# A graph layer by Strassen products on one core: VectorE's order written out, with sums of blocks two steps ahead

## The chip, the core and the metric

The kernel runs on one core of a Trainium2 chip. A core has five engines with a queue of instructions each: PE (TensorE, the matmuls), DVE (VectorE), ACT (ScalarE), POOL (GpSimd) and SP (SyncE). SP, ACT and POOL issue the DMAs. The metric is the device time of one execution in microseconds (us), the median of several runs. Beside it there is one profiled execution, whose instructions carry times; its span runs from the first to the last instruction.

## The reference, cut

There are 4096 nodes with 512 features in x, and a symmetric adjacency `adj` of 4096 x 4096 with nonzero values at some 0.8% of its places.

```python
# layer 0: a dense product with the scaled adjacency
h = relu(layernorm(x))
d = rowsum(adj) ** -0.5
x = x + relu((d[:, None] * adj * d[None, :]) @ h @ W0 + b0)
# layer 1: attention over the nonzero places, with both signs
h  = relu(layernorm(x))
hw = h @ W1
e  = leaky_relu(hw @ a[:512] + (hw @ a[512:]).T, 0.2)
p  =  softmax(where(adj > 0,  e, -1e12))
q  = -softmax(where(adj > 0, -e, -1e12))
x  = x + elu(concat([p @ h, q @ h], 1) @ wtrans)
```

## The kernel before, in words

**The work.** Layer 0 is done densely. `y0` holds h times W0, scaled by d, for all 4096 nodes in 32 tiles of 128 rows. The output's 32 row tiles are made in nine groups of four or two tiles: `GROUPS` is (28,4), (16,4), (26,2), (20,4), (0,4), (4,4), (8,4), (12,4), (24,2), as (first tile, number). Group 0 is an ordinary product that is done while x and adj are read and normalized, up to 312 us of the profiled span. Groups 1 to 8 (312 to 1059 us) use Strassen's method in Winograd's form: seven products in place of eight, over 16 steps `jp` of two row tiles of `y0` each. Layer 1 is sparse: per block of nodes it gathers the rows of a table (POOL, L473), and weights and sums them; it runs from group 8 to the end of the span.

**A step of a group** has these parts. `load_at` has SP load a block of adj. `sum_at` (L953) has DVE make four sums of its quarter blocks (L959 to L962) into a tile "sums", of which three buffers exist. `multiply_blocks` (L965) issues 28 matmuls of 128 x 256 (14 in a group of two tiles), all from L972. `pack` has ACT make the mask of nonzero places (L812), which POOL stores to the table (L821) once for two steps. In group 1 alone, `sum_y` (L938) also has DVE make the sums of the blocks of `y0`, which the later groups use again.

**The end of a group** is done during the next one. `take` is `join_blocks` (L846): DVE joins the seven products of a pair of tiles out of PSUM (L854 to L864), which frees the banks for the new group, and scales them (`affine`, L834). Then each finished row tile passes through `finish0` (L884): DVE adds x (L887), POOL stores the tile (L888, "x1d") and clears three columns of h (L889), DVE takes mean and variance and three small operations (L705, L706, L708) around a square root on ACT (L707), ACT makes h by a relu (L711), DVE makes two dot products with the attention vectors (L895), and the row tile is put in eight tables (L465): in one by POOL, in the seven others by ACT. h has two buffers. When all tiles of a group are through, `spread_s` (L907) turns their dot products on PE (L910, `s_ps`), and ACT copies and stores them.

**The lists.** For the sparse layer DVE also makes lists of nodes by class, in two halves (g = 1, then g = 0), each with seven classes. `list_round` (L397) finds eight entries with MAX8 (L410) and strikes them with MATCH_REPLACE (L412); a half has 73 rounds. A finished class gives a tile `li` (L425, two buffers), and eight `join`s (L428): indirect DMAs issued by POOL (L432), 56 for a half. `deal` (L439) has POOL fetch the whole list (L442), PE transpose it in three parts (L449) and DVE keep it (L450). `make_places` (L633) works out offsets, from a small product on PE (its DVE copy is L669).

**What sets the order.** The kernel is written in program order, and a scheduler sets the order of each engine's queue, except where `keep_in_program_order` fixes an instruction. `group` (L1118) is a loop over the steps: it prepares the blocks of step jp + 1, joins the former group at step 0, multiplies step jp, packs, finishes a tile of the former group in steps 0 to 3 (0 and 1 after a group of two), spreads s at step 12, and calls `step(jp)` (L1182), which takes so many pieces from the two lists `listing` and `joining`:

```python
n = 0 if b == 2 or not 0 < jp < 14 else 1 if b == 1 else 2 + jp % 2
for todo, n in ((listing, n), (joining, 1 + jp % 2)):
    for _ in range(n):
        if todo:
            todo.pop(0)()
```

Group 8 is called with other pools, after the lists are done.

Of the kernel before, what the change touches and what calls it, by code (L numbers as in the profile page):

```python
# [8 lines left out]
F32 = mybir.dt.float32  # L9
# [10 lines left out]
P = 128  # L20
# [12 lines left out]
NE = 8  # L33
# [234 lines left out]
def gcn_gat_kernel(  # L268
# [55 lines left out]
    def bank(name):  # L324
        return ps.tile([P, 512], F32, tag="ps", name=name)
# [112 lines left out]

    def deal(g):  # L439

        rows = make_pool.tile([P, EN], F32, tag="flag16", name=f"deal{g}")[:, : NH * STR // P]
        i = nc.gpsimd.dma_start(  # L442
            out=rows.rearrange("r (c p) -> r c p", p=P),
            in_=lst_dram[g].rearrange("(c r p) o -> r c (p o)", r=P, p=P),
        )
        turned = bank(f"deal_ps{g}")
        for c in range(NH * STR // P // P):
            part = slice(c * P, (c + 1) * P)
            nc.tensor.transpose(turned[:, part], rows[:, part], ident)  # L449
        nc.vector.tensor_copy(idx[g].rearrange("p b k -> p (b k)"), turned[:, : NH * STR // P])  # L450
        return i

# [107 lines left out]
    with sbuf(name="y0", bufs=1) as y_pool, sbuf(name="wa", bufs=1) as wa_pool, sbuf(name="bits", bufs=4) as bits_pool, sbuf(name="small0", bufs=4) as small, ExitStack() as rest, ExitStack() as lists:  # L560
# [65 lines left out]
        def count_nodes(g, kinds):  # L626

            one = make_pool.tile([P, EN], F32, tag="flag16", name=f"one{g}_{kinds[0]}")
            for c in kinds:
                nc.vector.tensor_scalar(one, codes[g], float(CODES[c]), None, ALU.is_equal)  # L630
                nc.vector.tensor_reduce(count[:, g, c : c + 1], one, AX.X, ALU.add)

        def make_places(g):  # L633


            o_ps = ps.tile([NH, NE + 1, NK + 1], F32, tag="ps", name=f"o_ps{g}")
            for e in range(NE + 1):
                nc.tensor.matmul(
                    o_ps[:, e, 0:NK], before[:, e, :], count[:, g], start=True, stop=True
                )  # L640
            o = make_pool.tile([NH, NE, NK], F32, tag="o", name=f"o{g}")
# [59 lines left out]
        def normalize(out, xt, name, pin=False):  # L701

            mv = mean_var(small, xt, name, pin)
            r = small.tile([P, 2], F32, tag="rr", name=f"rr{name}")
            nc.vector.tensor_scalar(r[:, 0:1], mv[:, 1:2], EPS, None, ALU.add)  # L705
            nc.vector.reciprocal(r[:, 0:1], r[:, 0:1])  # L706
            nc.scalar.activation(r[:, 0:1], r[:, 0:1], AF.Sqrt)  # L707
# [3 lines left out]
            return nc.scalar.activation(out, xt, AF.Relu, bias=r[:, 1:2], scale=r[:, 0:1])  # L711

# [4 lines left out]
        def turn_x(ln_pool, j, pin=False):  # L717

            hx = ln_pool.tile([P, F], F32, tag="hx", name=f"hx{j}", bufs=2)
            normalize(hx, xs.pop(j), f"a{j}", pin)  # L720
# [163 lines left out]
        def finish0(work, j, y, h, prod):  # L884
# [4 lines left out]
            nc.gpsimd.memset(h[:, ROW_T + 1 :], 0.0)  # L889
            i = normalize(h[:, :F], y, f"b{j}")  # L890
            if late0 <= j < late0 + n_late:
                tc.keep_in_program_order(i)

            def dot(g, vec):
# [12 lines left out]
        def spread_s(i0, n):  # L907

            rows = bank(f"s_ps{i0}")
            nc.tensor.matmul(rows[:n, :P], s_all[:, i0 : i0 + n], ident, start=True, stop=True)  # L910
            row = small.tile([6, P], F32, tag="s_row", name=f"s_row{i0}", bufs=1)
# [158 lines left out]
        listing, joining = [], []  # L1070
        verdict = None

        def make_lists(g):
            def rows_and_joins(c):
# [3 lines left out]
                if c == NK - 1:  # L1078
                    joining.append(partial(deal, g))
# [4 lines left out]
            listing.append(partial(make_places, g))  # L1084
            for n, (c, r) in enumerate(steps):
                listing.append(partial(list_round, g, n))
                if r + 1 == CAPS[c] // 8:
                    listing.append(partial(rows_and_joins, c))
# [28 lines left out]

        def group(b, work, at_pool, sum_pool, step, prod, n_h=2):  # L1118

            nonlocal pending  # L1120
# [4 lines left out]
            ats, sums = {}, {}  # L1125

            def prepare(jp):
                if 2 * jp % nj == 0:
                    ats[jp] = load_at(at_pool, i0, n, 2 * jp, nj)
                    sums[jp] = sum_at(sum_pool, ats[jp], n, f"sums{i0}_{jp}")  # L1130
                else:
                    ats[jp], sums[jp] = ats[jp - 1], sums[jp - 1]
                if b == 1:
                    sum_y(jp)

            prepare(0)
            for j in order[:2]:
                if j not in xrs:
                    load_xr(j)
            for jp in range(NP):  # L1140
                if jp + 1 < NP:
                    prepare(jp + 1)
                if jp == 0:
# [17 lines left out]
                if jp == NP - 4:  # L1161
# [11 lines left out]
        with sbuf(name="work0", bufs=2) as work, sbuf(name="sums", bufs=3) as sum_pool, sbuf(name="at", bufs=6) as at_pool:  # L1173
# [3 lines left out]

            for b in range(1, len(GROUPS) - 1):

                def step(jp):  # L1180
                    if jp == 4 and b == 1:
                        make_lists(1)  # L1182
                        make_lists(0)

                    n = 0 if b == 2 or not 0 < jp < 14 else 1 if b == 1 else 2 + jp % 2
                    for todo, n in ((listing, n), (joining, 1 + jp % 2)):
                        for _ in range(n):
                            if todo:
                                todo.pop(0)()

                group(b, work, at_pool, sum_pool, step, prod)
            while listing:
# [10 lines left out]
        with sbuf(name="work2", bufs=2) as work, sbuf(name="sums2", bufs=2) as sum_pool, sbuf(name="at2", bufs=4) as at_pool, sbuf(name="scratch", bufs=1) as scratch, sbuf(name="pair", bufs=1) as pair:  # L1203
# [75 lines left out]
            def step(jp):  # L1279
# [12 lines left out]
                if jp == NP - 1:  # L1292
# [3 lines left out]
                    )  # L1296

            group(len(GROUPS) - 1, work, at_pool, sum_pool, step, row_tile, 3)
            k = late0 % EJ
# [5 lines left out]
            for j, y in pending[1](work, row_tile).items():  # L1305
                finish0(work, j, y, late_h[:, j - late0], row_tile)
            weights0(blocks[1])
# [195 lines left out]
```

## Time and profile before

| | |
|---|---|
| runs | 2150.4, 2150.49, 2156.22 us; median 2150.49 |
| span of the profiled execution | 2033.7 us |
| between the span and the median | 116.8 us |
| busy share of the span: PE, DVE, POOL, ACT | 93%, 63%, 46%, 31% |
| mean granted TensorE clock | 0.976 |
| starts of groups 1 to 8 | 312.3, 420.5, 479.6, 588.4, 689.0, 787.3, 893.3, 1004.5 us |
| joins of the lists on POOL (L432) | 112, each 918 ns busy; 2.7 us from issue to landing in the median between 390 and 1000 us |
| fetches of the finished lists (L442) | at 598.6 and 965.4 us |

How to read it: the profiled execution's own time is given by its span; the run's time is longer by what lies around the span. A view lists "idle before" as the time in which an engine stood still just ahead of an instruction, with an arrow to what ended it. In the tables of stretches, each engine's busy time is followed by the number of its instructions, then come the granted clock (1.00 is full speed), the share of time the 16 DMA engines were busy, and GB/s.

### The profile page before, as it was taken

The page shows a single profiled execution, that of the slowest core. Times are in us where ns is not written, and L with a number is a line of the kernel's source. Part 1 is how long each engine was busy: PE and PEld are TensorE (multiplying, and loading weights), DVE is VectorE, ACT ScalarE, POOL GpSimd, SP SyncE. Part 2 cuts the span into 40 slices and gives each one's busy share as a digit, 9 for nine tenths or more (in the row PEclk, how much of TensorE's full clock was granted, in tenths as well). Part 3 has the DMA queues.
Part 4 walks back from the last instruction along what each step waited for, and adds up shares of the span by engine and source line. Part 5 has one row for each costly group of instructions (what it writes and reads, how often), then busy time and mean ns, then how long its engine had stood idle before and what let it go on. Part 6 is the DMA issues. An engine that isn't in the chain of part 4 may idle for free.

```text
span 2033.7 us, 23721 instructions
## 1 busy us (share of the span) xinstructions
PE 1884.8 (93%) x7832; PEld 1066.1 (52%) x7832; DVE 1279.9 (63%) x2907; ACT 626.0 (31%) x1181; POOL 932.4 (46%) x1047
## 2 busy tenths in 40 slices
PE   6999999897999999979996799999999999999998
PEld 3433337786788888868771233333333333333333
DVE  6555558989793538983354566566665656566653
ACT  5766652212112221212032233233322332333321
POOL 3000001133331113233064777777777777777770
PEclk9999999998999999989997899999999999999999
DMA  9988869467448565728384989989898898888880
GB/s 364 328 298 283 298 201 325 135 217 244 137 142 280 187 232 173 250 87 287 93 258 142 324 291 307 290 288 307 275 308 282 292 310 274 279 265 271 278 274 30
DMA packets 181115, 503.53 MB, mean 248 GB/s; under 512 B 27091, under 2 KB 35699, under 8 KB 180982
## 3 DMA queue, kind: packets, MB, share of 16 engines
q0 software_dynamic: 73184, 275.36, 42.1%
q1 hardware_dynamic: 77808, 171.80, 25.6%
q10 hardware_dynamic: 29990, 54.75, 7.7%
q8 instruction: 64, 1.05, 0.2%
q14 instruction: 69, 0.57, 0.1%
HBM read 409.89 MB, written 103.02 MB: 252 GB/s over the span
## 4 chain that ended last, share of the span: by engine, by line
POOL 16%; PE 13%; DMA 9%; issue 7%; DVE 4%; ACT 1%; DVEq 0%; POOLq 0%
POOL g L473 16%; DMA g<-table,idx 9%; PE u L516 7%; PE o L1397 5%; DVE p L509 1%; DVE z L487 1%; PE tp L550 1%; ACT p L499 1%; DVE z L1362 1%; ACT us L1383 0%; DMA table<-h 0%; DVE prod L895 0%; DVE stb L455 0%; DVE total L1367 0%; ACT y L1361 0%
## 5 line engine op out<-in xcount | busy, mean ns | idle before, releaser
L473 POOL DMA_INDIRECT g<-table,idx x704 | 701.4, 996 | 230.0 <-issue 209.3
L516 PE MATMUL u<-g,p 128*64 128x512 f32 x2816 | 628.6, 602 | 18.0 <-DVE p L509 13.2
L516 PEld LDWEIGHTS u<-g,p 128*64 128x64 f32 x2816 | 199.4, 139 | 394.1 <-issue 354.4
L972 PE MATMUL p<-t,sums 128*128 128x256 f32 x896 | 268.5, 384 | 15.2 <-DVE sums L960 10.4
L972 PE MATMUL p<-y,at 128*128 128x256 f32 x896 | 272.0, 386 | 3.6 <-DVE w L855 2.5
L487 DVE TENSOR_TENSOR z<-g,s 128x512 f32<-128x512 f32 (+1 forms) x124 | 78.4, 634 | 311.2 <-DMA g<-table,idx 298.1
L972 PE MATMUL p<-y,sums 128*128 128x256 f32 x896 | 270.6, 384 | 0.8 <-DVE sums L962 0.8
L1361 ACT ACTIVATE y<-z 128x512 f32<-128x512 f32 (+1 forms) x124 | 67.5, 544 | 553.1 <-DVE z L487 427.0
L1397 PE MATMUL o<-wt_sb,ut 128*128 128x512 f32 x512 | 228.3, 599 | 0.5 <-ACT ut L555 0.5
L432 POOL DMA_INDIRECT ld<-li,off x112 | 102.8, 918 | 258.7 <-DMA ld<-li,off 199.2
L812 ACT ACTIVATE m<-at 128x1024 uint8<-128x1024 f32 x110 | 115.0, 1053 | 339.7 <-DMA at<-in_adj_t 289.5
L1367 DVE TENSOR_REDUCE total<-p 128x128 f32<-128x1792 f32 x62 | 201.5, 3250 | 2.1
L972 PEld LDWEIGHTS p<-t,sums 128*128 128x128 f32 x896 | 171.8, 193 | 41.9 <-DVE sums L960 12.8
L972 PEld LDWEIGHTS p<-y,at 128*128 128x128 f32 x896 | 171.3, 193 | 32.1 <-DVE w L855 3.7
L972 PEld LDWEIGHTS p<-y,sums 128*128 128x128 f32 x896 | 173.1, 193 | 25.6 <-DVE sums L962 1.2
L509 DVE SCALAR_TENSOR_TENSOR p<-g,p 128x384 f32<-128x384 uint8 (+1 forms) x256 | 145.5, 619 | 23.3 <-ACT p L499 23.3
L821 POOL DMA_DIRECT2D table<-m x71 | 56.4, 795 | 220.3 <-ACT m L812 136.2
L747 ACT ACTIVATE junk<-ar 128x1024 bf16<-128x1024 f32 x128 | 134.7, 1052 | 72.1 <-DMA ar<-in_adj 70.8
L1397 PEld LDWEIGHTS o<-wt_sb,ut 128*128 128x128 f32 x512 | 96.0, 193 | 109.8 <-issue 108.9
L972 PE MATMUL p<-t,at 128*128 128x256 f32 x448 | 136.8, 388 | 9.6 <-DVE w L855 7.6
L499 ACT ACTIVATE p<-z 128x512 f32<-128x512 f32 (+2 forms) x252 | 123.6, 549 | 65.2 <-DVE z L1362 56.5
L776 PE MATMUL yp<-w_sb,hx_t 128*128 128x512 f32 x256 | 120.1, 613 | 2.9 <-DVE hx_t L729 2.9
(198 smaller groups left out, 1811.7 us busy)
## 6 DMA issues: line engine op xcount, KB each, us to landing
ar<-in_adj SPq DMA_DIRECT2D x128, 512.0 KB, 7.5
at<-in_adj_t SPq DMA_DIRECT2D x112, 512.0 KB, 4.1
table<-h ACTq DMA_DIRECT2D x182, 258.0 KB, 5.9
table<-m POOLq DMA_DIRECT2D x55, 256.0 KB, 4.9
g<-table,idx POOLq DMA_INDIRECT x704, 4.5
at<-in_adj_t SPq DMA_DIRECT2D x32, 256.0 KB, 7.8
xr<-in_x SPq DMA_DIRECT2D x32, 256.0 KB, 6.5
x1d<-y POOLq DMA_DIRECT2D x32, 256.0 KB, 5.3
```

The source lines that it names most:

```text
L432: return nc.gpsimd.indirect_dma_start(out=lst_dram[g][:, :], out_offset=bass.IndirectOffsetOnAxis(ap=off[g][:, e, c : c + 1], axis=0), in_ ...
L473: i = nc.gpsimd.indirect_dma_start(out=gt[:, k, :], out_offset=None, in_=table[2 * n // RPT], in_offset=bass.IndirectOffsetOnAxis(ap=idx[n ...
L487: return nc.vector.tensor_tensor(z, t.to_broadcast([P, n, RB]), s.unsqueeze(1).to_broadcast([P, n, RB]), ALU.add)
L499: i = nc.scalar.activation(p[:, :, :, g], z, AF.Exp, scale=(1.0, -1.0)[g])
L509: nc.vector.scalar_tensor_tensor(e, m, 0.0, e, ALU.is_gt, ALU.mult)
L516: i = nc.tensor.matmul(u[h * RB : (h + 1) * RB], p[:, k, h].rearrange("p g i -> p (g i)"), row(k), start=k == HALVES[r % 2][h][0], stop=en ...
L747: nc.scalar.activation(junk, ar, AF.Identity, accum_out=part[:, c : c + 1]),
L776: nc.tensor.matmul(yp, hx_t[j][:, c * P : (c + 1) * P], w0_sb[:, c, :], start=c == 0, stop=c == FC - 1,)
L812: nc.scalar.activation(m, at, AF.Sign)
L972: i = nc.tensor.matmul(out, left[:, x * P : (x + 1) * P], right, start=jp == 0 and first, stop=jp == NP - 1 and (final or not first),)
L1367: nc.vector.tensor_reduce(total, q, AX.X, ALU.add)
L1397: nc.tensor.matmul(po, ut[:, g, c, :], wt_sb[:, g * FC + c, :], start=g == 0 and c == 0, stop=g == 1 and c == FC - 1,)
```

## The change

In groups 1 to 7 the scheduler no longer orders DVE: its queue is in program order, by `tc.manual_schedule`. The program order is rewritten to suit:

- the blocks' loads and sums are made two steps ahead (`prepare(jp + 2)`), and in groups 1 to 6 the next group's first two at step 14 (`follow`), by a new function `preparer`; in a step they stand behind the multiplication and ahead of the tile that is finished;
- `finish0` and `normalize` become generators, so that a tile is finished in three pieces: up to the small operations ahead of the square root; the last small operation and the relu; the dots and the row's puts. The last piece of a tile stands behind the first piece of the next;
- in group 2, which has two tiles, the four tiles of the former group are finished at steps 2, 4, 6, 8 and not at 0 to 3;
- s is spread at step 9 (12 in group 2), in program order on PE;
- a list's `deal` is cut in three: the fetch, ten empty places later the transposes on PE in program order, two empty places later the copy on DVE; its tile has a place of its own;
- the product on PE in `make_places` is issued two rounds before the rest;
- rounds: group 1 one a step from step 3 to 13, group 2 one in every other step, group 3 up to three, later groups none or one in the first four steps, two in the fifth, then three; joins two a step.

The core of the diff:

```diff
-    def deal(g):
...
+                    wait = [lambda: None]
+                    joining.extend([fetch, *wait * 10, turn, *wait * 2, keep])
...
+        def preparer(b, at_pool, sum_pool):
+            i0, n = GROUPS[b]
+            nj = 8 // n
+            got = {}
+
+            def prepare(jp):
+                if 2 * jp % nj == 0:
+                    at = load_at(at_pool, i0, n, 2 * jp, nj)
+                    got[jp] = at, sum_at(sum_pool, at, n, f"sums{i0}_{jp}")
+                else:
+                    got[jp] = got[jp - 1]
+                if b == 1:
+                    sum_y(jp)
+
+            for jp in range(2):
+                prepare(jp)
+            return prepare, got
...
-            prepare(0)
+            prepare, got = ready
+            at_once = n == 4 or follow is None
+            when = {(k if at_once else 2 + 2 * k): k for k in range(pn)}
+            tail = None
...
             for jp in range(NP):
-                if jp + 1 < NP:
-                    prepare(jp + 1)
                 if jp == 0:
                     ys = take(work, prod)
...
-                multiply_blocks(acc, n, jp, ats[jp], sums[jp])
+                multiply_blocks(acc, n, jp, *got[jp])
                 if 2 * jp % nj == 0:
-                    pack(bits_pool, i0, 2 * jp, ats[jp])
-                if jp < pn:
-                    j = order[jp]
+                    pack(bits_pool, i0, 2 * jp, got[jp][0])
+                if jp + 2 < NP:
+                    prepare(jp + 2)
+                elif jp + 2 == NP and follow is not None:
+                    ready = follow()
+                if jp == (9 if at_once else 12):
+                    spread_s(p0, pn)
+                if jp in when:
+                    k = when[jp]
+                    j = order[k]
                     h = work.tile([P, ROW_W], F32, tag="h", name=f"h{j}", bufs=n_h)
-                    finish0(work, j, ys.pop(j), h, prod)
-                    if jp + 2 < pn:
-                        load_xr(order[jp + 2])
-                if jp == 12:
-                    spread_s(p0, pn)
+                    one = finish0(work, j, ys.pop(j), h, prod)
+                    next(one)
+                    if k + 2 < pn:
+                        load_xr(order[k + 2])
+                if tail is not None:
+                    next(tail, None)
+                    tail = None
+                if jp in when:
+                    next(one)
+                    tail = one
...
+            with tc.manual_schedule(engines={mybir.EngineType.DVE}):
+                ready = preparer(1, at_pool, sum_pool)
+                for b in range(1, len(GROUPS) - 1):
+
+                    def step(jp):
+                        if jp == 2 and b == 1:
+                            make_lists(1)
+                            make_lists(0)
+
+                        if b == 1:
+                            n = 1 if 2 < jp < 14 else 0
+                        elif b == 2:
+                            n = jp % 2 if 2 < jp < 14 else 0
+                        elif b == 3:
+                            n = min(jp, 3) if jp < 14 else 30 - 2 * jp
+                        else:
+                            n = (0, 1, 1, 1, 2)[jp] if jp < 5 else 3 if jp < 14 else 30 - 2 * jp
+                        for todo, n in ((listing, n), (joining, 2)):
...
```

More of the change, by code (lines that the diff above doesn't have):

```diff
@@ L437, in join, with fetch_lists @@
         )
-    def deal(g):
-        rows = make_pool.tile([P, EN], F32, tag="flag16", name=f"deal{g}")[:, : NH * STR // P]
-        i = nc.gpsimd.dma_start(
+    def fetch_lists(g):
+        rows = make_pool.tile([P, NH * STR // P], F32, tag="deal", name=f"deal{g}")
+        nc.gpsimd.dma_start(
             out=rows.rearrange("r (c p) -> r c p", p=P),
@@ L445, in deal, with turn_lists @@
         )
+        return rows
+    def turn_lists(g, rows):
         turned = bank(f"deal_ps{g}")
@@ L448, in deal, with keep_lists @@
             part = slice(c * P, (c + 1) * P)
-            nc.tensor.transpose(turned[:, part], rows[:, part], ident)
+            tc.keep_in_program_order(nc.tensor.transpose(turned[:, part], rows[:, part], ident))
+        return turned
+    def keep_lists(g, turned):
         nc.vector.tensor_copy(idx[g].rearrange("p b k -> p (b k)"), turned[:, : NH * STR // P])
-        return i
     def mean_var(pool, xt, name, pin):
@@ L631, in count_nodes, with sum_counts @@
                 nc.vector.tensor_reduce(count[:, g, c : c + 1], one, AX.X, ALU.add)
-        def make_places(g):
[L636 to L640, printed above, removed]
+        places, dealt = {}, {}
+        def sum_counts(g):
+            o_ps = places[g] = ps.tile([NH, NE + 1, NK + 1], F32, tag="ps", name=f"o_ps{g}")
+            for e in range(NE + 1):
+                tc.keep_in_program_order(
+                    nc.tensor.matmul(
+                        o_ps[:, e, 0:NK], before[:, e, :], count[:, g], start=True, stop=True
+                    )
+                )
+        def make_places(g):
+            o_ps = places.pop(g)
             o = make_pool.tile([NH, NE, NK], F32, tag="o", name=f"o{g}")
@@ L706, in normalize @@
             nc.vector.reciprocal(r[:, 0:1], r[:, 0:1])
-            nc.scalar.activation(r[:, 0:1], r[:, 0:1], AF.Sqrt)
+            yield nc.scalar.activation(r[:, 0:1], r[:, 0:1], AF.Sqrt)
             nc.vector.scalar_tensor_tensor(
@@ L710, in normalize @@
             )
-            return nc.scalar.activation(out, xt, AF.Relu, bias=r[:, 1:2], scale=r[:, 0:1])
+            yield nc.scalar.activation(out, xt, AF.Relu, bias=r[:, 1:2], scale=r[:, 0:1])
         def load_x(x_pool, queue, j):
@@ L719, in turn_x @@
             hx = ln_pool.tile([P, F], F32, tag="hx", name=f"hx{j}", bufs=2)
-            normalize(hx, xs.pop(j), f"a{j}", pin)
+            for _ in normalize(hx, xs.pop(j), f"a{j}", pin):
+                pass
             tp = bank(f"tx{j}")
@@ L889, in finish0 @@
             nc.gpsimd.memset(h[:, ROW_T + 1 :], 0.0)
-            i = normalize(h[:, :F], y, f"b{j}")
+            steps = normalize(h[:, :F], y, f"b{j}")
+            next(steps)
+            yield
+            i = next(steps)
             if late0 <= j < late0 + n_late:
                 tc.keep_in_program_order(i)
+            yield
             def dot(g, vec):
@@ L909, in spread_s @@
             rows = bank(f"s_ps{i0}")
-            nc.tensor.matmul(rows[:n, :P], s_all[:, i0 : i0 + n], ident, start=True, stop=True)
+            tc.keep_in_program_order(
+                nc.tensor.matmul(rows[:n, :P], s_all[:, i0 : i0 + n], ident, start=True, stop=True)
+            )
             row = small.tile([6, P], F32, tag="s_row", name=f"s_row{i0}", bufs=1)
@@ L1070, in gcn_gat_kernel @@
         listing, joining = [], []
-        verdict = None
+        verdict = ready = None
         def make_lists(g):
@@ L1078, in rows_and_joins, with fetch, turn, keep @@
                 if c == NK - 1:
-                    joining.append(partial(deal, g))
+                    def fetch():
+                        dealt[g] = fetch_lists(g)
+                    def turn():
+                        dealt[g] = turn_lists(g, dealt[g])
+                    def keep():
+                        keep_lists(g, dealt.pop(g))
+                    wait = [lambda: None]
+                    joining.extend([fetch, *wait * 10, turn, *wait * 2, keep])
             listing.extend(partial(block_codes, g, b) for b in range(2))
@@ L1083, in make_lists @@
             listing.extend(partial(count_nodes, g, k) for k in ((0, 1), (2, 3), (4, 5), (6,)))
-            listing.append(partial(make_places, g))
+            listing.append(partial(sum_counts, g))
             for n, (c, r) in enumerate(steps):
+                if n == 2:
+                    listing.append(partial(make_places, g))
                 listing.append(partial(list_round, g, n))
@@ L1116, in judge, with group @@
             return verdict
-        def group(b, work, at_pool, sum_pool, step, prod, n_h=2):
-            nonlocal pending
+        def preparer(b, at_pool, sum_pool):
[13 more added lines that the diff above has]
+            return prepare, got
+        def group(b, work, at_pool, sum_pool, step, prod, n_h=2, follow=None):
+            nonlocal pending, ready
             i0, n = GROUPS[b]
@@ L1124, in group @@
             order = [p0 + k for k in ((0, 2, 1, 3) if b > 1 and pn == 4 else range(pn))]
[L1125 to L1134, printed above, removed]
-            prepare(0)
+            prepare, got = ready
+            at_once = n == 4 or follow is None
+            when = {(k if at_once else 2 + 2 * k): k for k in range(pn)}
+            tail = None
             for j in order[:2]:
@@ L1176, in prod @@
                 return work.tile([P, F], F32, tag="q", name=name, bufs=1)
[L1178 to L1191, printed above, removed]
+            with tc.manual_schedule(engines={mybir.EngineType.DVE}):
[14 more added lines that the diff above has]
+                        for todo, n in ((listing, n), (joining, 2)):
+                            for _ in range(n):
+                                if todo:
+                                    todo.pop(0)()
+                    follow = None
+                    if b + 2 < len(GROUPS):
+                        follow = partial(preparer, b + 1, at_pool, sum_pool)
+                    group(b, work, at_pool, sum_pool, step, prod, follow=follow)
             while listing:
@@ L1296, in step @@
                     )
+            ready = preparer(len(GROUPS) - 1, at_pool, sum_pool)
             group(len(GROUPS) - 1, work, at_pool, sum_pool, step, row_tile, 3)
@@ L1305, in gcn_gat_kernel @@
             for j, y in pending[1](work, row_tile).items():
-                finish0(work, j, y, late_h[:, j - late0], row_tile)
+                for _ in finish0(work, j, y, late_h[:, j - late0], row_tile):
+                    pass
             weights0(blocks[1])
```

## The prediction

> **What bounds the kernel now.** I read the page first, then the busy table cut at the starts of the eight Strassen groups, then PE's waits, then POOL's and ACT's. The page gives the cost of a step: its three group rows on L972 that carry a sum of blocks or y show matmuls of 384 to 388 ns, two halves overlapped, and a step of a four-tile group (28 matmuls) repeats every 6.04 us in the trace, a step of a two-tile group (14) every 3.02 us. Sixteen steps are 96.6 and 48.3 us. The groups start at 312.3, 420.5, 479.6, 588.4, 689.0, 787.3, 893.3 and 1004.5 us, and group 8 ends at 1059.2. So each is longer than its steps by 11.5, 10.8, 12.2, 3.9, 1.6, 9.4, 14.5 and 6.3 us: **70.4 us** of loss. That is all a change of VectorE's order can win here.
>
> The busy table, one row a group (time stretch and length, then PE, PEld, DVE, ACT, POOL busy, granted clock, DMA share, GB/s):
>
> ```profile
> 312.00:420.00 108.00, 100.41 (x468) 86.24 (x467) 99.61 (x295) 24.81 (x29) 19.96 (x31) 0.97 0.65 219
> 480.00:588.00 108.00, 101.52 (x448) 87.29 (x448) 95.51 (x249) 20.16 (x22) 39.74 (x49) 0.95 0.50 155
> 588.00:689.00 101.00, 98.71 (x454) 85.18 (x453) 48.51 (x137) 20.57 (x25) 15.31 (x25) 1.00 0.66 217
> 689.00:787.00 98.00, 98.00 (x471) 85.62 (x470) 59.44 (x187) 20.68 (x25) 22.27 (x33) 1.00 0.65 216
> 787.00:893.00 106.00, 99.69 (x451) 85.57 (x451) 92.44 (x259) 20.57 (x25) 32.54 (x45) 0.98 0.61 199
> 893.00:1004.00 111.00, 101.33 (x456) 86.70 (x454) 47.63 (x139) 16.23 (x21) 29.59 (x41) 0.97 0.52 172
> ```
>
> DVE is full in groups 1, 3 and 6 (99.6, 95.5, 92.4 us) and half empty in 4, 5 and 7 (48 to 59). It is not short of time; the list rounds stand in the wrong groups and ahead of work PE needs. PE's waits from 300 to 1060 us say which (total, times, longest):
>
> ```profile
> PE p L972 <- DVE sums L960: 10.4, 6, 4.0
> PE p L972 <- DVE w L855: 10.0, 5, 6.9
> PE s_ps L910 <- DVE prod L895: 8.2, 1, 8.2
> PE s_ps L910 <- DVE o L669: 7.1, 1, 7.1
> PE p L972 <- DVE sums L961: 4.9, 1, 4.9
> ```
>
> The two s_ps rows are the s product standing in PE's queue before the dots are done (groups 1 and 2). The rows on sums are blocks summed late, w is a join late. These five rows are 40.6 us; much of the rest is half clock after the idle:
>
> ```profile
> 484.40:486.20 1.80, 1.13 (x4) 0.68 (x4) 1.80 (x5) 0.73 (x1) 1.50 (x4) 0.93 0.40 150
> 486.20:489.50 3.30, 3.07 (x8) 2.54 (x9) 3.30 (x7) 0.00 (x0) 2.13 (x4) 0.52 0.55 161
> 1007.00:1008.20 1.20, 0.34 (x2) 0.32 (x3) 1.20 (x4) 0.00 (x0) 0.00 (x0) 0.99 1.06 345
> 1008.20:1011.40 3.20, 3.20 (x9) 2.54 (x8) 3.20 (x8) 0.00 (x0) 0.00 (x0) 0.50 0.73 253
> ```
>
> Here the clock is 0.5 for 3.3 us after waits of 1.75 us (484.6) and 2.66 us (ending 1007.9); such a stretch costs half its length. So I add 1.7 us to a wait of 2 us or more, and 3.4 to one of 7 or more (6.8 us stretches follow those at 397 and 554).
>
> The Trainium skill, "TensorE: Matmul & The Clock Gate", Why this matters for your kernels, asks only that gaps stay under about 3 us. These two shorter gaps did cost a stretch, so the trace differs; by the page the additions on short waits would go, some 3 us of the sum.
>
> **The change, part by part.** T1 to T8 are the groups' starts.
>
> *The s product* moves to step 9 (or 12 for two-tile groups) in fixed place, where the dots of the last tile are past. Both waits go: 7.1 + 8.2, with clock some 19 us. Its copy and store on ACT go with it and nothing waits for them before the sparse layer.
>
> *Sums two steps ahead, joins ahead of tiles, lists behind both.* A set of four sums takes 4 x 0.42 us at most (0.335 by issue spacing), 1.5 us per 6.04 us step; the joins of four tiles take 6.0 us and four L834 rows 2.6; a tile's three pieces take 1.75, under 1, and 1.4 us. A list round is 1.3 us. In groups 4 to 7 the new rates put three rounds on a step: 1.5 + 3.9 = 5.4 of 6.04 us, which fits, and only from step 5 on, when the tiles are out. The late joins (4.5 in group 3, 3.4 in 4, 9.7 in 7) and late sums (some 7 in 3, 9 in 6, 2 in others) go, with their clock stretches.
>
> What comes in their place, group by group. Group 1: sums_1 and sum_y now stand ahead of the four L834, at_2 lands at 315.3, and PE gets the bank of the second tile pair only at some 319: a loss of 6 where step 0 lost 1.15; steps 6 and 7 hold sum_y, tiles and rounds and run over by 3 to 5 with clock. I take 10.7 (11.5 before). Group 2: tiles come every two steps, 6.04 us, but a tile's chain on ACT (seven puts of 5.5 us together, sqrt 0.2, relu 0.8, and dots between) takes some 8.3; three times 2.3 is 6.8, and I take 6.5 (10.8). Groups 3, 4, 6, 7: the short over-runs that even group 5 shows (1.6) and one of 1 to 2 us at the joins: 1.0, 2.7, 2.7, 3.8 (12.2, 3.9, 9.4, 14.5). These six are **27.4** against 62.3. They are estimates; each could be 2 us either way, more in group 1.
>
> *The joins of the lists on POOL.* This part speaks against the change. Each indirect store (L432) waits for the one before it to land:
>
> ```profile
> POOL ld L432 <- DMA ld<-li,off: 199.2, 91, 6.4
> ```
>
> and the price depends on the rest of the traffic. Three stretches, as first and last start (525 to 595, 882 to 910, and 882 to 962, which holds the second):
>
> ```profile
> L432 POOL DMA_INDIRECT ld<-li,off x24: 827/860/1398, 525.2 to 594.7; - x24
> L432 POOL DMA_INDIRECT ld<-li,off x12: 827/846/1082, 882.2 to 909.5; - x12
> L432 POOL DMA_INDIRECT ld<-li,off x24: 827/864/1368, 882.2 to 961.6; - x24
> ```
>
> That is 27.3/11 = **2.48** us apart at best; 69.5/23 = 3.02, or **2.8** without the 4.7 us that POOL waited for DVE there; and 79.4/24 = **3.3** while table rows are being put. The changed lists come later: the first list's classes 3 to 6 (32 joins) begin when the tiles of group 4 are out, about T4+41, and in POOL's built order all but the last few stand ahead of group 5's x1d of its first tile, all 32 ahead of that tile's row put (L465). There are two h buffers, so the third tile's relu waits for that put to land. POOL's time is 41 + 32p with p the price of a join; the put lands 7.5 us later (1.5 for POOL's own, 6 to land), and group 4 is 99.3 long: T5 + 32p - 50.8. Due is T5+29.5. Behind the relu, DVE stands in written order: dots of that tile, then sums_6. The sums two steps ahead cover some 3 us, and the clock takes as much. So p = 2.48 gives T5+28.6 and no loss; 2.8 gives 9.3 us; 3.3 gives 25.3, over the 1.6 that group 5 has now. In the old kernel the dots could be passed by sums on DVE, and g=1's joins were out by T4+6.
>
> The second list has the same at its end. Its classes 4 to 6 (24 joins) begin about T7+36, the fetch (L442) follows and lands 4.2 us after its issue as before, so +6 in all, and the three transposes of `turn` stand ahead of group 8's first matmul on PE. Group 7 is 100.4 long: PE waits 36 + 24p + 6 - 100.4 = 24p - 58.4, that is 1.1, 8.8 or 20.8 us, with 2 of clock in the two longer cases, over the 6.3 that group 8 loses now. The fetch was at 965.4 in the old run, 39 us before group 8; this cover is gone. Group 8's start moves everything after it: the chain of the sparse layer starts from its tiles and lists.
>
> The Trainium skill, "DMA: Bandwidth & Descriptors", Issuing engines are not separate DMA queues, says that issuing from several engines saves only the sequencers' time. Here the issuing engine decides: the seven puts of a tile on ACT went out at 441.7 to 447.1, and its eighth on POOL held the next relu for 12.1 us until 454.0. [...]
>
> **The sum.** With p = 2.8: 27.4 + (1.6 + 9.3) + (6.3 + 8.8 + 2) = 55.4 us of loss against 70.4: **-15**. I take 2.8, because in groups 4 and 7 the joins stand behind the tiles' puts, with only loads and masks beside them, as in 525 to 595, and DVE's lists are ahead of POOL. The span goes from 2033.7 to 2018.7. Around the profiled span lie 116.8 us to the median of 2150.49, which the change doesn't touch: **2135.5**.
>
> **The rivals.**
> - *POOL's joins never bite* (p = 2.48): 27.4 + 1.6 + 7.4 = 36.4, -34, **2116**. For it: the best stretch; against it: eight mask stores a group stand among the joins.
> - *POOL's joins become the bound*: p = 3.3 gives 27.4 + 26.9 + 29.1 = 83.4, +13, **2163.5**, slower. Its place is the h buffer of group 5 and the transposes at T8. Loss moves by 56 us for each us of p, so it decides above p = 2.8 + 15/56 = 3.07, and gain within 0.3% (6.5 us, about what a measurement of this kernel can tell) lies at 2.95 to 3.18. For it: 3.3 was the price of the second list's last joins; against it: rows were being put then.
> - *The tiles' chain on ACT is late in every four-tile group* (8.3 against 6.04): 2.3 us for three tiles behind the first, in groups 3 to 7, less the 3 us of cover: up to 4 a group, 20 in all, **2155**, no change. Against it: with steps of 6.04 the sums of two steps are already made.
> - *It doesn't do what it says*: DVE's order is written, but PE, ACT and POOL are still ordered by the scheduler; then the s product or the joins stay where they were and 20 to 30 us of the win go: **2160**.
>
> **How the numbers follow.** The forecast and its neighbours 0.33, fast rival 0.17, POOL bound 0.27, ACT chain 0.13, not as said 0.10. Faster than 2144 holds most of the first and all of the second: 0.47. Within 2144 to 2157: part of the first, the ACT chain and the edge of the bound: 0.20. Slower: 0.33. The range 2112 to 2172 takes both ends of p with a few us for the group estimates; the forecast's own, p from 2.65 to 2.95, is 2127 to 2144.
>
> **What would show it.** Right: no PE wait on the s product; steps of 6.04 in groups 3, 4, 6 and 7; in group 5 one PE wait near step 6 behind an ACT relu that waits for a row put; at T8 PE waits for the transposes with POOL's fetch a few us before. Wrong: PE waits at sums or w in groups 3 to 7 (DVE's order does not fit), joins over 3.07 us apart, or groups 1 and 2 over 14 and 10 us of loss.

## The result, and the profile after

The changed kernel takes **2165.26 us** in the median (2161.51 to 2169.96, 6 runs) where the kernel before takes 2153.35 (2150.4 to 2157.46, 6 runs): ratio 1.0053, 95% interval 1.0028 to 1.0077. It is slower, by 11.9 us in the medians. The forecast was 2135.5, faster. The rival "POOL's joins become the bound" had 2163.5.

All executions of that measurement, of both kernels, were some 6% longer than those of the experiments below, and the first profile of before, with its span of 2033.7, is of the shorter kind where that of after (2161.7) is of the longer. So I compare the Strassen groups, whose step is 6.04 us in both, and ratios; and I repeated both kernels. Run beside the kernel before on one chip, the changed kernel takes 2038.79 against 2031.51 us, ratio 1.0044 (1.0026 to 1.0062).

The changed kernel by its own group starts: groups 1, 3, 4, 5, 6, 7 (stretch, busy PE, PEld, DVE, ACT, POOL, clock, DMA share, GB/s):

```profile
311.20:418.90 107.70, 101.42 (x469) 87.02 (x468) 87.65 (x241) 24.81 (x29) 14.18 (x24) 0.97 0.66 217
476.40:573.60 97.20, 97.20 (x451) 85.12 (x450) 80.15 (x207) 18.98 (x21) 26.28 (x35) 1.00 0.51 159
573.60:672.20 98.60, 97.48 (x451) 85.05 (x450) 81.72 (x218) 20.47 (x25) 27.01 (x38) 1.00 0.66 216
672.20:801.00 128.80, 104.49 (x472) 88.82 (x471) 95.89 (x257) 20.58 (x25) 37.24 (x49) 0.88 0.53 170
801.00:900.20 99.20, 97.50 (x451) 85.06 (x451) 83.92 (x225) 20.68 (x25) 29.84 (x42) 1.00 0.63 212
900.20:1016.00 115.80, 98.51 (x454) 85.36 (x452) 65.82 (x175) 16.29 (x21) 32.61 (x48) 0.96 0.55 179
```

DVE's work is spread as intended: 80 to 84 us in groups 3, 4 and 6, where it was 95, 48 and 92. Groups 3, 4 and 6 are 97 to 99 us long, close to their 96.6 us of steps. But group 5 is 128.8 us long where it was 98, and group 7 is 115.8. Losses of groups 1 to 8 over their steps, in us (the sums are taken before rounding):

| kernel | 1 | 2 | 3 | 4 | 5 | 6 | 7 | 8 | sum |
|---|---|---|---|---|---|---|---|---|---|
| before, first profile | 11.5 | 10.8 | 12.2 | 3.9 | 1.6 | 9.4 | 14.5 | 6.3 | 70.4 |
| before, repeated | 13.3 | 12.0 | 7.8 | 5.2 | 1.6 | 8.4 | 17.6 | 6.3 | 72.2 |
| after, first profile | 11.1 | 9.2 | 0.6 | 2.0 | 32.2 | 2.5 | 19.2 | 16.6 | 93.3 |
| after, repeated | 13.1 | 9.4 | 0.6 | 2.5 | 29.5 | 5.3 | 18.7 | 5.3 | 84.4 |

PE's waits in the changed kernel, 300 to 1060 us (total, times, longest):

```profile
PE p L991 <- DVE sums L979: 32.8, 7, 21.1
PE deal_ps L452 <- DMA deal<-ld: 13.8, 1, 13.8
PE p L991 <- DVE t L965: 6.3, 3, 3.6
PE p L991 <- DVE sums L978: 2.8, 1, 2.8
```

The 7 to 8 us on the s product are gone, and those on w. Two new waits outweigh them: one of 21.1 us on sums, and 13.8 us at the transposes. The row on sums names DVE, but DVE was not busy; it was itself waiting. Where that began is on ACT in group 5 (start, length, engine and line; in brackets the idle time before and what ended it):

```profile
696.44 5.41 ACTq L470 DMA_DIRECT2D table<-h  x7
725.57 0.81 ACT L723 ACTIVATE h<-y,rrb 128x512 f32<-128x512 f32 x1 [29.15 <-DMA table<-h]
```

The third tile's relu stands 29.15 us, until a row put has landed and its h is free. ACT's own puts of the first tile were out by 694.5. The last put of that tile is POOL's:

```profile
691.57 0.85 POOL L432 DMA_INDIRECT ld<-li,off  x1 [1.11 <-DMA ld<-li,off]
697.58 1.02 POOL L432 DMA_INDIRECT ld<-li,off  x1 [5.15 <-DMA ld<-li,off]
705.29 0.83 POOL L432 DMA_INDIRECT ld<-li,off  x1 [6.70 <-DMA ld<-li,off]
...
716.50 0.60 POOL L901 DMA_DIRECT2D x1d<-y  x1
...
722.24 0.86 POOL L432 DMA_INDIRECT ld<-li,off  x1 [0.75 <-DMA ld<-li,off]
723.11 0.61 POOL L470 DMA_DIRECT2D table<-h  x1
```

POOL issues it (L470) at 723.11, straight behind the last join of the first list, and the relu runs 2.5 us later. The group began at 672.2, so x1d of its first tile is issued 44 us after the group's start. While ACT issues its puts the joins go slower (6.0 and 7.7 us apart at 691 to 705), and the joins hold back the put that ACT needs.

### The profile page after: what moved, and what is told of

It is laid out like the page before. It is cut to its first block, busy times and chain, and to the rows that moved or that the text cites. A ratio compares the mean times of both kernels' runs of the same rounds, so it can differ in the third digit from the quotient of the medians.

```text
span 2161.7 us, 23708 instructions
## 1 busy us (share of the span) xinstructions
PE 1957.5 (91%) x7832; PEld 1085.2 (50%) x7832; DVE 1317.3 (61%) x2907; ACT 633.2 (29%) x1181; POOL 928.1 (43%) x1047
## 4 chain that ended last, share of the span: by engine, by line
PE 38%; issue 6%; POOL 3%; DVE 2%; DMA 1%; another core or an unknown queue 1%; ACT 0%; DVEq 0%; POOLq 0%
PE u L521 25%; PE o L1463 9%; POOL g L478 3%; PE p L991 2%; PE tp L555 2%; DMA g<-table,idx 1%; DVE p L514 1%; PE cs L545 0%; DVE z L492 0%; DVE eo L1471 0%; DVE z L1428 0%; DVE total L1433 0%; DVE eo L1475 0%; DVE y L1474 0%
## 5 line engine op out<-in xcount | busy, mean ns | idle before, releaser
L521 PE MATMUL u<-g,p 128*64 128x512 f32 x2816 | 697.6, 619 | 79.6 <-issue 64.8
L521 PEld LDWEIGHTS u<-g,p 128*64 128x64 f32 x2816 | 216.9, 141 | 505.4 <-issue 479.1
L1471 DVE TENSOR_SCALAR eo<-o 128x512 f32<-128x512 f32 x32 | 22.1, 691 | 262.6 <-remote 101.6
L1449 ACT ACTIVATE us<-u,rl 128x512 f32<-128x512 f32 x62 | 42.6, 688 | 351.4 <-remote 127.0
L492 DVE TENSOR_TENSOR z<-g,s 128x512 f32<-128x512 f32 (+1 forms) x124 | 77.8, 629 | 92.2 <-DMA g<-table,idx 74.2
```

The source lines that it names most:

```text
L492: return nc.vector.tensor_tensor(z, t.to_broadcast([P, n, RB]), s.unsqueeze(1).to_broadcast([P, n, RB]), ALU.add)
L521: i = nc.tensor.matmul(u[h * RB : (h + 1) * RB], p[:, k, h].rearrange("p g i -> p (g i)"), row(k), start=k == HALVES[r % 2][h][0], stop=en ...
```

## The experiments

All times are beside the kernel before on the same chip, whose medians in the four sets were 2034.7, 2031.5, 2029.7 and 2032.7 us.

### Both kernels again

No edit.

> The kernel before, unchanged, for a profile beside the others. The first profile had a span of 2033.7 us where its runs take some 2150. Theory (the Strassen groups decide the change): the groups lose 70 us here as in the first profile, to within 5, and what is longer lies in the sparse layer. Rival: this run's groups lose 80 or more, so that the change took less from them than the two profiles say (93.3 after against 70.4).

> The changed kernel, unchanged, beside the others. Theory: the loss of the groups is 80 to 95 us against 72 before (group 5 some 30, the transposes' wait 10 to 15 at the end of group 7), and the time is over the kernel before by that difference, +8 to +20. Rival (the end of group 8 and the sparse layer made the difference where the change was first measured): the loss is 75 to 80 and the time within 5 us of before.

Measured: 72.2 us of loss before and 84.4 after, and 2038.8 against 2031.5 us. The losses are those of the first theory in both. The time is not quite: +7.3 us, where +8 to +20 was expected. The two profiles, which come from different chips, show the same: 12.2 us of loss became 7.4 us in the spans (2039.1 against 2031.7), because the time behind group 8 was 973 us before and 968 after; why stays open. (In the first profile of after it was 1081, with the groups alike but for group 8; that stays open too.) And group 8 of the first profile of after lost 16.6 us because its last two steps took 7.7 and 9.6 us with PE idle in ten short pieces that have no releaser; in the repeated profile they take 3.02. That part belongs to that execution.

### A third h buffer

```diff
-                    group(b, work, at_pool, sum_pool, step, prod, follow=follow)
+                    group(b, work, at_pool, sum_pool, step, prod, 3, follow=follow)
```

> The changed kernel with three h buffers in groups 1 to 7. Theory (in group 5 the row put of tile 0 stands behind all joins of the first list on POOL, and the third tile's relu waits for it): now the fourth tile's relu waits for it, one step of 6.04 us later, so the PE wait moves from step 6 to step 7 and group 5's loss falls from 32.2 to about 26; time -6 us against the changed kernel's 2165. Rival (the chain of puts on ACT is what is late): a third buffer lets ACT run ahead, the wait in group 5 falls under 8 us, time -25. The wait for the transposes at group 8 stays within 4 us of 13.8 by both.

Measured: 2032.82 us, ratio 0.9996 (0.9974 to 1.0018). The wait moved from step 6 to step 7 and group 5's loss fell to 24.4 us. ACT shows why:

```profile
704.03 0.81 ACT L723 ACTIVATE h<-y,rrb 128x512 f32<-128x512 f32 x1 [5.96 <-DMA table<-h]
731.86 0.81 ACT L723 ACTIVATE h<-y,rrb 128x512 f32<-128x512 f32 x1 [25.50 <-DMA table<-h]
```

The third relu now goes at 704, and the fourth stands 25.5 us for the same put, which POOL issues at 729.4. So it is POOL's put and no lateness of ACT's own; a buffer buys one step. The wait at the transposes was 9.3 us, a little below what both accounts allowed.

### POOL's order written out

```diff
-            with tc.manual_schedule(engines={mybir.EngineType.DVE}):
+            with tc.manual_schedule(engines={mybir.EngineType.DVE, mybir.EngineType.Pool}):
...
-                        for todo, n in ((listing, n), (joining, 2)):
+                        for todo, n in ((listing, n), (joining, 0 if b == 5 and jp < 5 else 2)):
```

> The changed kernel with POOL's order in groups 1 to 7 written out too, and no joins given out in the first five steps of group 5, so that the last eight joins of the first list stand behind the tiles' row puts. Theory: 24 joins at 3.43 us from T4+42 end at T5+26, the put of tile 0 follows at once and lands by T5+33, 3.5 us late instead of 24: group 5 loses 4 to 8 us instead of 32; the wait for the transposes stays 10 to 18 us; time -20 to -28 against 2165. Rival (ACT's puts and the DMA engines, not POOL's order, make the relu late): group 5 still loses over 20, time within 8 us of 2165.

Measured: 2040.8 us, ratio 1.0033 (1.0012 to 1.0054): no gain. Group 5's loss did fall, from 29.5 to 14.2, not to 4 to 8: the 24 joins ended at T5+18, even before the theory's T5+26, but POOL, now in written order, waits itself, 6.4 us for the landing of a put ahead of clearing the next h (L902), with the next put behind. And group 6 lost 17.0 (5.3 in the changed kernel's repeat), because joins of the second list now stand between its puts. So over half of group 5's loss goes with the joins; the fix moved the rest into POOL's own waits.

### List rounds earlier

```diff
-                            n = jp % 2 if 2 < jp < 14 else 0
+                            n = 1 if 0 < jp < 14 else 0
...
-                            n = (0, 1, 1, 1, 2)[jp] if jp < 5 else 3 if jp < 14 else 30 - 2 * jp
+                            n = (0, 1, 1, 1, 2)[jp] if jp < 5 else 3 if jp < 14 else 2
```

> The changed kernel with list rounds earlier: group 2 one a step from step 1, and groups 4 to 7 two in step 15 as well. By the built order the joins of the first list that stand ahead of group 5's puts are 24 instead of 32, and for the second list 24 stand ahead of group 7's first put and only 8 are left for group 7's end. Theory: group 5 loses 5 to 10 instead of 32, group 7 gains a wait of 10 to 25 us at step 6, the wait for the transposes at group 8 goes (0 to 2 instead of 13.8); time -10 to -30 against 2165. Rival (joins are not what holds the puts): group 7 has no wait at step 6 and group 5's stays over 20.

Measured: 2033.56 us, ratio 1.0007 (0.9986 to 1.0027). The pattern is in the main the one expected: the wait at the transposes is gone (the second list is fetched at 979.9, not 1011.3), group 5 loses 15.3, and group 7 has a new step 6 of 21.1 us, because the joins now stand ahead of its puts. But groups 4 and 6 rose too, to 8.8 and 9.5 (2.5 and 5.3 in the repeat), group 5 lost more than the 5 to 10 expected, and the sum is 81.1. Moving the joins in time moves the collision from group to group.

### Nothing of a tile on POOL

```diff
-            nc.gpsimd.dma_start(out=x1_dram[j], in_=y)
-            nc.gpsimd.memset(h[:, ROW_T + 1 :], 0.0)
+            nc.sync.dma_start(out=x1_dram[j], in_=y)
+            nc.vector.memset(h[:, ROW_T + 1 :], 0.0)
...
-            put_row(nc.gpsimd, tab0, j, h)
+            put_row(nc.scalar, tab0, j, h)
```

> The changed kernel with nothing of a finished tile left on POOL: the row put of table 0 goes to ACT with the seven others, x1d to SP, the three columns of h are cleared by DVE. POOL keeps joins, fetches and masks. Theory (only POOL's order holds the tiles): group 5 loses under 6 us instead of 32; in group 7 the joins start 7 us earlier and the transposes wait 4 to 10 us instead of 14; the groups lose 45 to 52 in all; time -20 to -28 against the kernel before. Rival (the eighth put on ACT, 0.8 us a tile, makes ACT's chain the bound): groups 3 to 7 each lose 3 to 6 us, the gain is under 10.

> As the one with the queues apart, and two list rounds in step 15 of groups 4 to 7, so that the second list is done some three steps earlier. Theory: the transposes' wait goes (0 to 2 us), DVE has room in step 15 (two rounds are 2.6 us); the groups lose 38 to 46 us, time -26 to -34 against the kernel before, a further -5 to -8 against the queues apart alone. Rival: the two rounds delay the joins of blocks at the next group's start, 2 to 4 us in each of four groups, and nothing is won.

The second adds to the first only the last edit of the experiment before (two rounds in step 15). Measured: 2046.12 us, ratio 1.0074 (1.0054 to 1.0094), and 2043.42, ratio 1.0053 (1.0029 to 1.0077). Both theories fell and the rival's pattern came, larger than I had it: group 5 fell from 29.5 to 9.0, but groups 1, 4, 6 and 7 rose by 4 to 7 us each, all at steps 5 and 6. ACT in group 4 of the first:

```profile
601.71 5.48 ACTq L470 DMA_DIRECT2D table<-h  x8
607.23 0.81 ACT L723 ACTIVATE h<-y,rrb 128x512 f32<-128x512 f32 x1 [5.92 <-DMA table<-h]
...
615.02 4.47 ACTq L470 DMA_DIRECT2D table<-h  x8
619.59 0.81 ACT L723 ACTIVATE h<-y,rrb 128x512 f32<-128x512 f32 x1 [4.96 <-DVE y L900]
...
627.06 4.47 ACTq L470 DMA_DIRECT2D table<-h  x8
631.64 0.81 ACT L723 ACTIVATE h<-y,rrb 128x512 f32<-128x512 f32 x1 [4.02 <-DMA table<-h]
```

The relus are 12.2 us apart, and tiles are due every 6.04: ACT's eight puts, then a landing, then the relu. The tiles' chain is the next bound behind POOL, but not by ACT's eighth put alone. The same edit has DVE clear the columns of h, in written order, and the dots of the tile before stand behind that:

```profile
613.10 0.06 DVE L902 MEMSET h<- 128x3 f32 x1 [7.68 <-DMA xr<-in_x]
```

The buffer to be cleared is that of the tile whose puts ACT issued at 601.7 to 607.2; the last issued landed at 612.9 (the view names another DMA, which came a little later). The second tile's relu ended at 608.0, and its dots, which its puts need, began only at 614.3; in the changed kernel's group 5 ACT began that tile's puts 1.9 us after its relu began, here 7.8. So some 6 of the 12.2 us are DVE's wait at the clear, and no run has the put and the clear moved apart. With two rounds in step 15, the transposes' wait went, and groups 5 and 6 lost more at step 0 (11.7 and 9.5 us): the gain and the price cancel, as its rival said.

### The s product alone, on the kernel before

```diff
-            nc.tensor.matmul(rows[:n, :P], s_all[:, i0 : i0 + n], ident, start=True, stop=True)
+            tc.keep_in_program_order(
+                nc.tensor.matmul(rows[:n, :P], s_all[:, i0 : i0 + n], ident, start=True, stop=True)
+            )
...
-                if jp == 12:
+                if jp == (9 if n == 4 else 12):
```

> The kernel before with one part of the change alone: the s product at step 9 (12 in groups of two tiles), in fixed place on PE. Theory: PE's waits on the s product in groups 1 to 3 (28 us in the repeated profile) go with 4 to 6 us of clock; nothing else moves; the groups lose 48 to 56 instead of 72, time -14 to -24 against the kernel before. Rival (the waits only pass to the sums behind): the PE waits on sums grow by over 10 us and the gain is under 10.

Measured: 2023.54 us, ratio 0.9958 (0.9942 to 0.9974), loss 66.3. Faster, by 8 us where 14 to 24 were expected. A part of the gap is a misreading in the expectation: of its 28 us of waits on the s product, 9.6 are at 1083.7, behind group 8 and outside what the edit moves. Group 1 loses 2.0 us instead of 13.3, but group 2 loses 23.0 instead of 12.0: its step 0 takes 13.2 us and its s product at step 12 still waits 9.8. There PE now waits 7.5 us at step 0 for a join (w, L855): the waits pass on, as the rival had it, but not to sums (9.7 us of waits on these, 12.9 without the edit). This part of the change is a gain by itself.

### The transposes later

```diff
-        rows = make_pool.tile([P, NH * STR // P], F32, tag="deal", name=f"deal{g}")
+        pool = make_pool if g else const
+        rows = pool.tile([P, NH * STR // P], F32, tag="deal", name=f"deal{g}")
...
-                    joining.extend([fetch, *wait * 10, turn, *wait * 2, keep])
+                    if g:
+                        joining.extend([fetch, *wait * 10, turn, *wait * 2, keep])
+                    else:
+                        joining.append(fetch)
+                        later.extend([turn, keep])
...
+                if jp in (6, 8):
+                    later.pop(0)()
```

The last two lines stand in the step of group 8.

> The changed kernel with the second list's transposes on PE moved from the start of group 8 to its step 6, and their copy on DVE to step 8 (that list is first read in the second half of the sparse layer). Theory (PE stands 11 to 14 us at the transposes and loses 2 to 4 more at half clock): that wait goes, the groups lose 68 to 73 us instead of 84, time -11 to -16 against the changed kernel's 2039, some 2025 where the kernel before has 2032. Rival (the wait hides other work of group 7's end that comes to light): group 8's step 0 grows from 7.8 to over 12 us and the gain is under 6.

Measured: 2032.56 us, ratio 1.0013 (0.9994 to 1.0032), loss 77.8 instead of 84.4. The wait at the transposes is gone, and group 8's step 0 takes 17.5 us where it took 7.8: the rival. DVE stands in the middle of the joins of blocks (990 to 1020 us) while POOL ends the list:

```profile
DVE y L878 <- issue: 8.4, 1, 8.4
```

```profile
1006.03 0.80 POOL L443 DMA_DIRECT2D deal<-ld  x1 [1.38 <-DMA ld<-li,off]
```

DVE goes on at 1006.11, when the last join has landed (1005.7). Group 8 has pools of its own, laid over the memory of the lists; that this is the reason was tried last, below. The transposes were one of two locks on the same door.

### Tiles every second step

To the last: the tiles of the former group at steps 0, 2, 4, 6.

```diff
-            when = {(k if at_once else 2 + 2 * k): k for k in range(pn)}
+            when = {(2 * k if n == 4 else k if at_once else 2 + 2 * k): k for k in range(pn)}
...
-                            n = (0, 1, 1, 1, 2)[jp] if jp < 5 else 3 if jp < 14 else 30 - 2 * jp
+                            n = (0, 1, 1, 2, 2, 2, 2, 2)[jp] if jp < 8 else 3 if jp < 14 else 30 - 2 * jp
```

> As the one before, and the four tiles of the former group are finished at steps 0, 2, 4, 6 and not at 0 to 3 in every four-tile group, with the list rounds of groups 4 to 7 as 0, 1, 1, 2, 2, 2, 2, 2 in the first eight steps. Theory (a tile's chain through ACT needs 8 us or more where the steps give 6): groups 6 and 7 lose under 2.5 each beside their end, and group 1's losses at steps 5 to 7 (7 to 9 us) go; group 5, where 16 joins of the first list and more now stand ahead of the puts, still loses 8 to 20 of its 30; groups 45 to 58 in all, time 2005 to 2018. Rival (spreading the tiles moves the joins ahead of still more puts): group 5 loses 25 or more and groups 4 and 6 get waits of their own, no gain over the one before.

> All three: tiles at steps 0, 2, 4, 6, their puts, stores and clears off POOL, the transposes in group 8. Theory (joins ahead of puts on POOL, then eight puts in a row on ACT, then the transposes are all that the written order lost in groups 4 to 8): groups 4 to 7 lose under 3 each, group 8 some 5, group 1 8 to 12, group 2 9 to 11; 36 to 44 in all, time -24 to -32 against the kernel before (2000 to 2008). Rival (DVE itself is full: 35 rounds, sums, joins and tiles leave it no slack in a group of 97 us): groups 4 to 7 lose 5 or more each on sums, time within 15 of before.

The second has nothing of a tile on POOL as well. Measured: **2012.06 us**, ratio 0.9904 (0.987 to 0.9937), and **2005.22**, ratio 0.9867 (0.9826 to 0.9907). Groups 3, 4, 6 and 7 lose 0.6 us each in both, group 5 8.1 and 7.5. So with twice the time for a tile, and the list rounds spread to match (the two were not tried apart), the tiles' chain holds nothing in these groups, and POOL's order costs little. The 7 us between the two kernels don't lie in groups 1 to 8, which lose some 52 us in both, and their intervals overlap. The first theory holds. The second holds in time (2000 to 2008 was expected) but not in its sum: 52.4 us instead of 36 to 44, since the door of group 8 now shows in full, step 0 of 26.9 and 25.0 us. Group 7 had hidden part of it in waits of its own. In the second kernel the profile names what DVE's first work on the new pools waited for, the last join, issued at 981.21:

```profile
981.21 0.83 POOL L432 DMA_INDIRECT ld<-li,off  x1 [1.34 <-DMA ld<-li,off]
983.40 0.06 DVE L903 MEMSET h<- 128x3 f32 x1 [16.57 <-DMA ld<-li,off]
```

### The lists' memory free

To the last kernel:

```diff
-        li = make_pool.tile([P, max(CAPS)], F32, tag="li", name=f"li{g}_{c}", bufs=2)
+        if g == 0 and c > NK - 4:
+            li = const.tile([P, CAPS[c]], F32, name=f"li{g}_{c}")
+        else:
+            li = make_pool.tile([P, max(CAPS)], F32, tag="li", name=f"li{g}_{c}", bufs=2)
```

> As the one with tiles spaced, queues apart and transposes late, and the last three li tiles of the second list lie in memory of their own, not in the pool that group 8's pools are laid over. Theory (group 8's step 0 of 25 us there, and of 17.5 with late transposes alone, is DVE's first instruction on the new pools waiting for the last join to have read its li): step 0 of group 8 falls to 7 to 10 us, the groups lose 34 to 40 instead of 52, time 1985 to 1995 where the kernel before has 2030. Rival (another tile or another engine's wait stands behind it, the fetch or a mask store): step 0 stays over 18, time within 6 of 2005.

Measured: **1998.37 us**, ratio 0.984 (0.9812 to 0.9869), loss 44.3 (34 to 40 expected). Group 8's step 0 falls to 9.7 us: the theory's mechanism holds. The time misses its range by 3 us, for a wait came up at step 6 (13.8 us): DVE stands 11.9 us until 993.2 ahead of a dot (L916). The view names no releaser; POOL's queue at that time:

```profile
989.23 0.81 POOL L446 DMA_DIRECT2D deal<-ld  x1 [1.36 <-DMA ld<-li,off]
990.02 1.57 POOL L838 DMA_DIRECT2D table<-m  x2
```

It was not the list's fetch, which landed at 991.9, but fits the first of the two mask stores behind it, which landed at 993.1: in group 8 the dots write to a tile of the masks' pool (`row_tile`), and POOL issues these two stores behind the joins and the fetch. So it seems to be once more something that stands behind the joins in POOL's order; giving the dots a tile elsewhere was not tried. This is the fastest kernel of the study, ahead of the kernel before and of the changed one. Three of its groups (3, 4, 6):

```profile
472.00:569.00 97.00, 97.00 (x450) 85.01 (x449) 80.44 (x209) 19.09 (x21) 27.05 (x32) 1.00 0.51 162
569.00:666.00 97.00, 97.00 (x451) 85.03 (x450) 82.05 (x220) 20.25 (x25) 22.31 (x26) 1.00 0.67 219
769.00:866.00 97.00, 97.00 (x450) 85.03 (x449) 80.79 (x222) 20.47 (x25) 24.82 (x29) 1.00 0.67 219
```

PE is busy without a gap at full clock, with DVE at 80 to 82 of 97 us: the written order is sound. What spoiled the change were the queues beside it.

## Why the prediction was wrong

It named the right places and chose the wrong one of its prices: 2.8 us for a join of the lists, where 3.43 was measured. Point by point:

- **What can be won** (70.4 us; 72.2 repeated): right. That 116.8 us lie "around the span" was wrong: a repeated run of before has a span of 2031.7 for 2033.52 us. The sum of losses stood; the 116.8 us were the difference between two measurements.
- **The s product**: right; in groups 1 and 2 PE no longer waits on it. Group 2 lost 9.2 and 9.4 us instead of the forecast 6.5. The forecast's reason, the tiles' chain on ACT, shows at step 12, which takes 8.0 and 10.5 us: PE waits 2.8 and 5.2 us for sums that stand in DVE's order behind a tile that waits for ACT. In the first profile:

```profile
458.57 0.16 DVE L720 SCALAR_TENSOR_TENSOR rrb<-mvb,rrb 128x1 f32<-128x1 f32 x1 [4.21 <-ACT rrb L719]
```

- **The late sums and joins of groups 3, 4, 6, 7**: right in the main. Groups 1 to 4, 6 and 7 without its last step lose 29.1 us in the first profile (forecast 27.4), 36.5 in the repeat, against 62.3 before.
- **Group 5**: this is the step that failed. "I take 2.8, because in groups 4 and 7 the joins stand behind the tiles' puts, with only loads and masks beside them ..." The 32 joins began at T4+42 (forecast 41), and took from 615.8 to 722.2 us, 106.4/31 = **3.43** us each (3.37 in the repeat). The first two stood beside the rest of group 4's puts (7.3 and 5.3 us apart), and the last ten ran into group 5's own (6.0 and 7.7), because even at 2.8 they end at T5+32, past the start of those puts. The calm that I took for the price could not last by my own sum. The twenty between, beside loads and masks only, were 3.16 us apart, 2.97 without POOL's waits for DVE, so a part of the miss lay in the calm price too. Group 5 lost 32.2 and 29.5, not 10.9. At 3.43 the formula gives 31.1. The joins as the profile lists them:

```profile
L432 POOL DMA_INDIRECT ld<-li,off x32: 832/845/1357, 615.8 to 722.2; - x32
```

- **The transposes at group 8**: right in place, low in size: 13.8 and 11.4 us instead of 8.8. The 24 joins were 3.09 apart (937.8 to 1008.8). I did not see the second lock, the pools that lie over the lists; without the transposes it alone holds group 8.
- **The sum**: with 3.43 and 3.09 in the two formulas it is 27.4 + 31.1 + 24.1 = 82.6, against 84.4 measured and 72.2 before. That it comes so near is partly luck: the six groups lost 36.5 and not 27.4, and the end of group 7 with group 8 lost 18.4 and not 24.1. Still the rival "POOL's joins become the bound" was the right account. Its mechanism is shown by the third h buffer (the wait moves with the buffer), by the earlier lists (the wait moves with the joins) and by the puts taken off POOL (group 5's loss falls from 29.5 to 9.0). Its number, 2163.5 for 2165.26, is partly luck too: its 3.3 is 79.4 us over 24 joins, but these have 23 gaps, which makes 3.45, and with that it would have said 2172.
- **The tiles' chain on ACT**: less than forecast while POOL is the bound (groups 4 and 6: 2 to 5 us). When POOL is freed the tiles' chain is the next bound, there with DVE's clear of h in it as well; spacing the tiles, with the list rounds to match, removes it.

## What to carry to other kernels

When work is spread evenly over an engine that had slack, look at what its results set off on the other queues: a serial chain of DMAs that starts later collides with what comes next, and a queue in order passes that on. Price such a chain at the traffic that it will run beside, its own lateness included; if its end falls into a busy stretch, the calm price is not to be had. And before removing a wait on one instruction, list everything else that waits for the same event, pool memory too.

## What the runs showed of the hardware

- Indirect stores that each wait for the one before were 2.19 to 2.22 us apart where hardly anything else moved, and 6.0 and 7.7 us apart while rows were being put and the DMA engines were full; that the traffic is the reason is read from this and was not tried apart. Two stretches of the changed kernel, 692 to 702 and 712 to 722 us (the DMA share is the last number but one):

```profile
692.00:702.00 10.00, 10.00 (x48) 8.81 (x47) 9.59 (x27) 1.85 (x3) 1.44 (x2) 1.00 1.03 346
712.00:722.30 10.30, 0.00 (x0) 0.00 (x0) 0.00 (x0) 0.00 (x0) 5.53 (x9) 0.52 0.19 64
```

  In the second, PE, DVE and ACT all stand still.
